# Deep and own blocks of a sparse graph attention in turns, and several steps of its schedule queued elsewhere

## The chip, the cores and the metric

The kernel runs on one core of a Trainium2 chip. That core has five engines: TensorE (PE, with its weight loads shown apart as PEld), VectorE (DVE), ScalarE (ACT), GpSimd (POOL) and SyncE (SP, which here issues transfers only). The metric is the time of one execution on the device in microseconds (us), as the median of several runs.

## The reference

It is one layer of multi-head attention over a fixed graph, with a residual and a layer norm: 16 batches of 1024 nodes with 512 features, 8 heads of 64, everything in float32. The adjacency `adj` (1024 x 1024, zeros and ones) is the same for all batches and sparse, and its rows have very different lengths.

```python
q = (x @ Wq + bq).reshape(b, n, H, HD)
k = (x @ Wk + bk).reshape(b, n, H, HD)
v = (x @ Wv + bv).reshape(b, n, H, HD)
scores = jnp.einsum('bqhd,bkhd->bhqk', q, k) / jnp.sqrt(jnp.float32(HD))
scores = scores + (1.0 - adj)[None, None, :, :] * -1000000000.0
attn = jax.nn.softmax(scores, axis=-1)
out = jnp.einsum('bhqk,bkhd->bqhd', attn, v).reshape(b, n, d)
x = _layernorm(x + out @ Wo + bo, axis=-1)
```

A row without any neighbour gets the average of all v. The random graph is an input, so the kernel finds its neighbours on the chip.

## The kernel before

**Tiles and blocks.** The 1024 nodes are ranked by their number of neighbours and cut into 8 tiles of 128. Instead of a dense product of scores, the kernel walks over neighbours: a *block* is 128 pairs of a query and a key. For a block, POOL gathers the keys' rows of k and v (1024 numbers each, tile `kvg`) from memory, DVE multiplies q with k (`products`, L1251) and adds up each head (`scores`, L1255), ACT takes the exponentials (`exponentials`, L1266), and v is multiplied with them (`weigh`): by ACT in eight small instructions, one for each head (L1276), or by DVE in one (L1280). `by_act` says which.

There are two kinds. In an *own* block every partition holds one of its own queries (the i-th neighbour of each), so that DVE simply adds it to the tile's sum (`add_own`, L1292); the first one of a tile starts the sum. `OWN = (2, 1, 2, 3, 4, 5, 5, 7)` gives their number by tile. What longer rows have beyond that is packed into *deep* blocks, `BLOCKS = (0, 0, 0, 0, 0, 0, 1, 5)`. A deep block's partitions belong to arbitrary queries, so it needs a second gather (`qg`, L1184), and PE adds it up with a matrix of zeros and ones (`add_up`, L1301 and L1302, into a PSUM tile with one buffer). A batch has 32 or 34 blocks, all batches together 530. Tile 1 has one key and no blocks. From batch 2 on, batches go in pairs: the odd one ("merged") also does the tile 0 of both.

**The written-out schedule.** The order of the instructions on every engine comes from one loop over steps `n` (L1470 on), some 39 steps ahead of block 0 up to 12 after the last. Each engine then runs its own instructions in that order and waits for the others by semaphores. In step n the loop queues the exponentials of block n+3, the products of n+4, gathers up to block n+8 (`AHEAD`; 11 ahead once the fronts are done), DVE's weighing of n+1, ACT's of n+2, and the sum of n. `later(k, fn)` puts a piece of work k steps ahead. The gathers of a batch may only be queued once `set_up` has the batch.

**PE's units.** PE's products are cut into units, with a credit for each step (`share`, paced by `load_of`). `fronts` are the projections of coming batches: `pair(b, j)` does q, k and v for two tiles of x. The k and v products follow a scheme with seven half products for eight, in units of four PE records: x, p6, x again, p7, z, p4, z again. Banks x and z have one buffer, and the second use waits for ACT's copy `e` (L960) or DVE's `out_v1` (L975). Between them stand the query products `q0` and `q1` (`pq`, L790) and the transposes `xt` of coming x tiles (`pxT`, L748). `finish` is the output product of a tile (`po`, also L790), and `complete` its residual and layer norm: spread (ACT), variance (DVE), power (POOL, L1113), shift (DVE), norm_out (ACT), store (POOL, L1125). `urgent` holds single PE pieces that go ahead of units: transposes of finished tiles and `mean_pe` (`pm`, L858), the average of v. Its row is copied by ACT (L862) and stored by SP (L864), and that is what sets `set_up`.

**What the change also touches.** `load_x` gathers a tile of x (L1001; three buffers) on POOL. `bias_setup` and `edges` are generators that run one piece at each step, in the lead-in: they fold bv into the output's bias (`pb`, L419) and make the lists of the deep blocks (`poff`, L675). The y tiles of `complete` have six buffers. While fronts last, kvg has eight.

Of the kernel before, what the change touches and what calls it, by code (L numbers as in the profile page):

```python
# [177 lines left out]
def kernel(  # L178
# [37 lines left out]
    B, N, D = x.shape  # L216
# [37 lines left out]
    with ExitStack() as main:  # L254
# [139 lines left out]
        def bias_setup():  # L394
            bk_bc = work.tile([P, D], F32, tag="y", name="bk_bc", bufs=Y_BUFS)
            broadcast(bk_bc, bk)
            yield
            n4 = small.tile([P, NPAIR], F32, name="bk_norms", bufs=1)
            nc.vector.tensor_tensor(bk_bc, bk_bc, bk_bc, op=OP.mult)
            nc.vector.tensor_reduce(n4, bk_bc.rearrange("p (h d) -> p h d", d=P), axis=AX.X, op=OP.add)  # L400
            nc.vector.tensor_reduce(bk_norm, n4, axis=AX.X, op=OP.max)
            n8 = small.tile([P, HEADS], F32, name="bq_norms", bufs=1)
            nc.vector.tensor_tensor(bk_bc, bq_bc, bq_bc, op=OP.mult)
            nc.vector.tensor_reduce(n8, bk_bc.rearrange("p (h d) -> p h d", d=HD), axis=AX.X, op=OP.add)
            nc.vector.tensor_reduce(bq_norm, n8, axis=AX.X, op=OP.max)
            yield
            pb = fill_psum("pb")
            nc.tensor.transpose(pb[:, 0:2 * NPAIR], bias_rows, ident[:2 * NPAIR, :2 * NPAIR])
            nc.tensor.transpose(pb[:, 2 * NPAIR:3 * NPAIR], bv_rows, ident[:NPAIR, :NPAIR])
            yield  # L410
            nc.vector.tensor_copy(bias_qk, pb[:, 0:2 * NPAIR])
            bv_col = one.tile([P, NPAIR], F32, name="bv_col")
            nc.vector.tensor_copy(bv_col, pb[:, 2 * NPAIR:3 * NPAIR])
            bvb = work.tile([P, NPAIR, P], F32, tag="y", name="bvb", bufs=Y_BUFS)
            nc.vector.tensor_copy(bvb, bv_col[:, :, None].to_broadcast([P, NPAIR, P]))
            yield
            pb = fill_psum("pb3")
            for c in range(NPAIR):
                nc.tensor.matmul(pb, bvb[:, c, :], W["o"][:, c, :], start=(c == 0), stop=(c == NPAIR - 1))  # L419
            yield  # L420
            nc.vector.tensor_tensor(bo_bc, pb, bo_bc, op=OP.add)
# [20 lines left out]
        def later(k, fn):  # L442
            plan.setdefault(now[0] + k, []).append(fn)
# [187 lines left out]
        def edges(t):  # L631
# [38 lines left out]
                nc.vector.tensor_tensor(check[:, 2 * NT + 1:2 * NT + 2], ranked[:, t, 1:2], st[:, 0:1], op=OP.subtract)  # L670

            nc.vector.tensor_scalar(deg, ranked[:, t, 1:2], -float(K), 0.0, op0=OP.add, op1=OP.max)
            yield
            po = fill_psum(f"poff_{t}")
            nc.tensor.matmul(po[:, 0:1], before, deg, start=True, stop=True)  # L675
            yield
# [66 lines left out]
        def transpose_x(b, t):  # L743
            def pe():
                xs = X.pop((b, t))
                p = fill_psum(f"pxT_{b}_{t}")
                for c in range(NPAIR):
                    nc.tensor.transpose(p[:, ts(c, P)], xs[:, ts(c, P)], ident)  # L748

                def out():  # L750
                    XT[b, t] = work.tile([P, D], F32, tag="xT", name=f"xT_{b}_{t}", bufs=4)
                    nc.scalar.copy(XT[b, t], p)
                    n = b * NT + t + 3
                    if t == 0 and b >= PAIRED_FROM:
                        if not merged(b):
                            BOTH[b // 2] = work.tile([P, 2, NPAIR, P], F32, tag="place", name=f"both_{b}", bufs=1)
                        nc.scalar.copy(
                            BOTH[b // 2].rearrange("p w c (h n) -> p h c w n", h=2)[:, b % 2],
                            p.rearrange("p (c w n) -> p c w n", c=NPAIR, w=2),
                        )  # L760
                        sq = work.tile([P, D], F32, tag="ysq", name=f"sq_x_{b}", bufs=1)
                        nc.scalar.activation(sq[0:LONE, :], xs[0:LONE, :], AF.Square, accum_out=x_norm[0:LONE, b:b + 1])
                    if b * NT + t in STORED:
                        nc.sync.dma_start(residual[b * NT + t], xs)
                        later(2, lambda: load_x(n // NT, n % NT))
                    else:
                        load_x(n // NT, n % NT)
                    if t % 2 and (b, t) != (0, 1):
                        later(1, combine)

                def combine():
                    s = [work.tile([P, HD2], F32, tag=f"s{i}", name=f"s{i}_{b}_{t}", bufs=1 + i // 4) for i in (1, 2, 3, 4)]
                    x0, x1 = XT[b, t - 1], XT[b, t]
                    nc.vector.tensor_tensor(s[0], x1[:, 0:HD2], x1[:, HD2:D], op=OP.add)
                    nc.vector.tensor_tensor(s[2], x0[:, 0:HD2], x1[:, 0:HD2], op=OP.subtract)
                    nc.vector.tensor_tensor(s[1], s[0], x0[:, 0:HD2], op=OP.subtract)
                    nc.vector.tensor_tensor(s[3], x0[:, HD2:D], s[1], op=OP.subtract)
                    SX[b, t // 2] = s

                later(1, out)  # L780

            return [(TRANSPOSE, pe, lambda: (b, t) in X)]
# [24 lines left out]
        def pair(b, j):  # L807
# [25 lines left out]
            def send(i):  # L833
# [8 lines left out]
                if R["sent"] == 2:  # L842
                    later(1, add_v)
                    if j == NT // 2 - 1:
                        later(2, lambda: urgent.append(mean_pe))

            def add_v():
                kv = [KV.pop((b, t))[:, D:] for t in tt]
# [133 lines left out]
            def s(i):  # L982
                return lambda: SX[b, j][i - 1]

            units = []
            units += unit("x", lambda: a(0, 0), B11, True, out_e, None)
            units += unit("p6", s(2), T2, True, out_w, None)
            units += q0
            units += unit("x", lambda: a(0, 1), B21, False, lambda: out_k(0, R["x"]), "e")
            units += unit("p7", s(3), T3, True, out_g, None)  # L990
# [94 lines left out]
        def complete(b, t, p, plain):  # L1085
# [46 lines left out]
            if single:  # L1132
                late = 1 if fronts else 0
                later(2 + late, variance)
                later(3 + late, power)
                later(4 + 2 * late, shift)
                later_last(5 + 2 * late, norm_out)
            elif second:
                later(3, variance)
                mate_shift, mate_norm_out = half.pop()[1]  # L1140
# [29 lines left out]


        KG, QG, PV, PSUM, QT, RDEN, V1 = {}, {}, {}, {}, {}, {}, {}
        blocks = [(b, t, i) for b in range(B) for t in tiles_of(b) if t != ONE_KEY for i in range(OWN[t] + BLOCKS[t])]
        start = [min(n for n, block in enumerate(blocks) if block[0] == b) for b in range(B)] + [len(blocks)]

        def load_more():
# [90 lines left out]

        def by_act(n):
            b, t, i = blocks[n]
            return 0 < i < OWN[t] or n < total - NBT and (n % 2 == 0 or n < NBT // 2)  # L1270

        def weigh(n):
            v, pv = KG.pop(n), PV[n]
# [174 lines left out]
        with tc.manual_schedule():  # L1448
# [21 lines left out]
            while n < total or plan or rest or urgent or done or finishing or spilled or lone_tiles or not guarded:  # L1470
# [50 lines left out]
                    reload(*spilled.pop(0), reloads)  # L1521
                    reloads, last_reload = reloads + 1, n
                first_unit = True
                while credit > 0 or urgent:
                    if urgent and not (first_unit and fronts):
                        urgent.pop(0)()
                        continue
                    if (
# [2 lines left out]
                    ):  # L1531
                        finishing = finish(*done.pop(0))
                        last_finish = n
                    units = finishing or fronts
                    if not units:
                        if urgent:
                            urgent.pop(0)()
# [52 lines left out]
```

## Time and profile before

| | us |
|---|---|
| median of 3 runs | 1903.44 (1902.83 to 1912.35) |
| the profiled execution | 1892.33 |
| its span, first to last instruction | 1890.4 |
| mean granted TensorE clock | 0.989 |
| PE / DVE / ACT / POOL busy | 1815.1 / 1700.6 / 1531.7 / 1267.4 |

The profile is of one execution. Busy time is the union of an engine's instructions; idle time in front of an instruction is put down to whatever released it last. In a row of the waits, the first number is the total in us, then follow how often, and the longest. The row of a group ends with its busy time, the mean ns of one instruction, and the idle time before them. All rows of PE count two records for one float32 matrix product.

### The profile page before, as it was taken

Reading aid. Unit: us, or ns where it says so; the run is one execution under the profiler, and the core shown is the slowest. Engines: PE = TensorE matmul, PEld = TensorE weight load, DVE = VectorE, ACT = ScalarE, POOL = GpSimd, SP = SyncE. Lnnn points to the kernel's source line nnn. Section 1 sums busy time; section 2 is a strip of 40 time slices with the busy share of each in tenths; the row PEclk is TensorE's granted clock in tenths of the full one; section 3 lists DMA queues with packets and bytes.
Section 4 is the critical chain, followed back from the end, with each engine's and each line's share of the span. In section 5 each row is a group of like instructions: output and inputs, shape, how many; then the busy total and the mean of one; then the engine's idle time right before and its main releaser. Section 6 shows DMA issues by size and latency. Waiting matters only on the chain. (4 is left out here: it accounts for less than half of the span.)

```text
span 1890.4 us, 25101 instructions
## 1 busy us (share of the span) xinstructions
PE 1815.1 (96%) x5149; PEld 878.2 (46%) x5149; DVE 1700.6 (90%) x3484; ACT 1531.7 (81%) x6016; POOL 1267.4 (67%) x1189
## 2 busy tenths in 40 slices
PE   7989999999999999999999999999999999999995
PEld 3434444444545454444445444444445444444442
DVE  6888889999999999899899989899999999997874
ACT  3627869979888988979798978989898989886794
POOL 1367766777677676757677676767666777656774
PEclk9989999999999999999999999999999999999997
DMA  7357787988889898888889898999889899989993
GB/s 280 114 168 226 233 307 227 315 295 294 308 287 316 305 328 283 305 288 307 312 292 335 271 334 274 314 304 310 301 307 326 293 356 310 314 277 340 334 319 117
DMA packets 188149, 544.63 MB, mean 288 GB/s; under 512 B 32602, under 2 KB 32622, under 8 KB 187986
## 3 DMA queue, kind: packets, MB, share of 16 engines
q0 software_dynamic: 116400, 382.82, 60.6%
q1 hardware_dynamic: 68510, 154.30, 21.8%
q10 hardware_dynamic: 3076, 5.82, 0.9%
q14 instruction: 120, 0.98, 0.2%
q8 instruction: 43, 0.70, 0.1%
HBM read 419.52 MB, written 144.34 MB: 298 GB/s over the span
## 5 line engine op out<-in xcount | busy, mean ns | idle before, releaser
L1276 ACT ACTIVATE pv<-kvg,pv 128x64 f32<-128x64 f32 x3432 | 864.6, 340 | 0.0
L1230 POOL DMA_INDIRECT kvg<-kv_pair,place_row x462 | 526.7, 1140 | 258.0 <-ACT pv L1276 73.3
L790 PE MATMUL po<-wo,oT 128*128 128x512 f32 x816 | 380.1, 596 | 1.0 <-ACT oT L1340 0.9
L790 PE MATMUL pq<-wq,xT 128*128 128x512 f32 x792 | 368.9, 597 | 0.4 <-DVE g L966 0.4
L1255 DVE TENSOR_REDUCE s<-qk 128x8 f32<-128x512 f32 x530 | 360.2, 680 | 7.5
L1251 DVE TENSOR_TENSOR qk<-qt,kvg 128x512 f32<-128x512 f32 x434 | 296.4, 683 | 22.2 <-DMA kvg<-kv_pair,place_row 22.1
L947 PE MATMUL pp<-t,s 128*128 128x512 f32 x504 | 237.4, 593 | 2.7 <-ACT sq_k L800 1.7
L947 PE MATMUL x<-b,xT 128*128 128x512 f32 x504 | 237.8, 594 | 0.8 <-ACT e L960 0.8
L790 PEld LDWEIGHTS po<-wo,oT 128*128 128x128 f32 x816 | 152.6, 191 | 166.8 <-issue 153.9
L1292 DVE TENSOR_TENSOR pv<-pv,pv 128x520 f32<-128x520 f32 x329 | 228.0, 693 | 0.7 <-ACT pv L1276 0.6
L790 PEld LDWEIGHTS pq<-wq,xT 128*128 128x128 f32 x792 | 149.2, 192 | 166.4 <-issue 155.0
L1266 ACT ACTIVATE pv<-s,absent 128x8 f32<-128x8 f32 x434 | 126.3, 293 | 79.8 <-DVE s L1255 76.2
L1001 POOL DMA_INDIRECT x<-in_x_dram,asked_row x120 | 130.2, 1085 | 88.3 <-PE pxT L748 40.5
L1125 POOL DMA_INDIRECT out_dram<-y,asked_row x129 | 144.8, 1122 | 35.7 <-issue 19.8
L800 ACT ACTIVATE sq_k<-kv 128x128 bf16<-128x128 f32 x512 | 150.9, 301 | 6.0 <-DVE kv L970 6.0
L947 PEld LDWEIGHTS pp<-t,s 128*128 128x128 f32 x504 | 94.2, 190 | 114.1 <-issue 101.4
L947 PEld LDWEIGHTS x<-b,xT 128*128 128x128 f32 x504 | 94.3, 191 | 111.5 <-issue 106.5
L1184 POOL DMA_INDIRECT qg<-q_rows,query_row x96 | 106.9, 1114 | 36.5 <-issue 24.7
L947 PE MATMUL z<-b,s 128*128 128x512 f32 x252 | 119.1, 595 | 6.5 <-DVE kv L975 6.5
L1029 POOL DMA_INDIRECT y<-in_x_dram,asked_row x93 | 104.5, 1124 | 27.5 <-issue 25.8
L947 PE MATMUL z<-t,s 128*128 128x512 f32 x252 | 120.0, 599 | 0.0
L947 PE MATMUL pp<-t,xT 128*128 128x512 f32 x252 | 118.4, 592 | 0.0
(276 smaller groups left out, 2766.7 us busy)
## 6 DMA issues: line engine op xcount, KB each, us to landing
kv_pair<-kv SPq DMA_DIRECT2D x98, 512.0 KB
q_rows<-q SPq DMA_DIRECT2D x106, 256.0 KB
qt<-q_rows SPq DMA_DIRECT2D x98, 256.0 KB
residual<-x SPq DMA_DIRECT2D x36, 256.0 KB
y<-residual SPq DMA_DIRECT2D x36, 256.0 KB
kv_rows<-kv SPq DMA_DIRECT2D x15, 512.0 KB
kvg<-kv_pair,place_row POOLq DMA_INDIRECT x462, 6.5
kv_pair<-kv SPq DMA_DIRECT2D x28, 256.0 KB
```

The source lines that it names most:

```text
L790: nc.tensor.matmul(p, lhs(c), w[:, c, :], start=(c == 0), stop=(c == NPAIR - 1))
L800: nc.scalar.activation(sq, s[:, ts(h, P)], AF.Square, scale=scale, accum_out=sums[:, h:h + 1])
L947: nc.tensor.matmul(R[bank], l[:, ts(c, P)], right[:, c, :], start=(first and c == 0), stop=(c == 1), skip_group_check=True,)
L1001: nc.gpsimd.indirect_dma_start(out=y, out_offset=None, in_=x_rows, in_offset=bass.IndirectOffsetOnAxis(ap=asked_row[:, t:t + 1], axis=0), ...
L1125: nc.gpsimd.indirect_dma_start(out=out_rows[b, t], out_offset=bass.IndirectOffsetOnAxis(ap=rows, axis=0), in_=y, in_offset=None, element_o ...
L1184: nc.gpsimd.indirect_dma_start(out=q, out_offset=None, in_=q_rows[b % ROWS], in_offset=bass.IndirectOffsetOnAxis(ap=rows, axis=0))
L1230: nc.gpsimd.indirect_dma_start(out=KG[n], out_offset=None, in_=rows, in_offset=bass.IndirectOffsetOnAxis(ap=(place_row if b else key_row)[ ...
L1251: nc.vector.tensor_tensor(QK[n], q, KG[n][:, 0:D], op=OP.mult)
L1255: nc.vector.tensor_reduce(S[n], QK.pop(n).rearrange("p (h d) -> p h d", d=HD), axis=AX.X, op=OP.add)
L1266: nc.scalar.activation(PV[n][:, D:], S.pop(n), AF.Exp, bias=bias)
L1276: nc.scalar.activation(pv[:, ts(h, HD)], v[:, ds(D + h * HD, HD)], AF.Copy, scale=pv[:, D + h:D + h + 1])
L1292: nc.vector.tensor_tensor(PV[b, t], PV[b, t], pv, op=OP.add)
```

## The change

Eight edits:

- `blocks_of`: in batches 1 to 15 the deep blocks of a tile are put between its own blocks, tile 7 as 0 1 D 2 D 3 D 4 D 5 D 6, tile 6 as 0 1 2 D 3 4. The first block of a tile stays first.
- `by_act`: a deep block's engine now goes by the parity of batch and number (`b + i`) instead of the parity of its place in the whole order.
- the product of the average of v is queued four steps after the second v tile instead of two;
- `bias_setup` and `edges` wait two steps more ahead of their products;
- a gather of x is queued one step later;
- in `complete`, while fronts last, power, shift and norm_out are queued one step later;
- in each batch's first pair, one x transpose takes the place of the first query product, and the query products and the other transpose stand between z's two uses;
- in the last three steps that have blocks, no units are queued, only urgent pieces.

```diff
--- before.py
+++ after.py
@@ -413,7 +413,8 @@
             nc.vector.tensor_copy(bv_col, pb[:, 2 * NPAIR:3 * NPAIR])
             bvb = work.tile([P, NPAIR, P], F32, tag="y", name="bvb", bufs=Y_BUFS)
             nc.vector.tensor_copy(bvb, bv_col[:, :, None].to_broadcast([P, NPAIR, P]))
-            yield
+            for _ in range(3):
+                yield
             pb = fill_psum("pb3")
             for c in range(NPAIR):
                 nc.tensor.matmul(pb, bvb[:, c, :], W["o"][:, c, :], start=(c == 0), stop=(c == NPAIR - 1))
@@ -670,7 +671,8 @@
                 nc.vector.tensor_tensor(check[:, 2 * NT + 1:2 * NT + 2], ranked[:, t, 1:2], st[:, 0:1], op=OP.subtract)
 
             nc.vector.tensor_scalar(deg, ranked[:, t, 1:2], -float(K), 0.0, op0=OP.add, op1=OP.max)
-            yield
+            for _ in range(3):
+                yield
             po = fill_psum(f"poff_{t}")
             nc.tensor.matmul(po[:, 0:1], before, deg, start=True, stop=True)
             yield
@@ -764,7 +766,7 @@
                         nc.sync.dma_start(residual[b * NT + t], xs)
                         later(2, lambda: load_x(n // NT, n % NT))
                     else:
-                        load_x(n // NT, n % NT)
+                        later(1, lambda: load_x(n // NT, n % NT))
                     if t % 2 and (b, t) != (0, 1):
                         later(1, combine)
 
@@ -842,7 +844,7 @@
                 if R["sent"] == 2:
                     later(1, add_v)
                     if j == NT // 2 - 1:
-                        later(2, lambda: urgent.append(mean_pe))
+                        later(4, lambda: urgent.append(mean_pe))
 
             def add_v():
                 kv = [KV.pop((b, t))[:, D:] for t in tt]
@@ -985,6 +987,8 @@
             units = []
             units += unit("x", lambda: a(0, 0), B11, True, out_e, None)
             units += unit("p6", s(2), T2, True, out_w, None)
+            if j == 0:
+                q0, q1, xt = xt[:1], q0 + xt[1:], []
             units += q0
             units += unit("x", lambda: a(0, 1), B21, False, lambda: out_k(0, R["x"]), "e")
             units += unit("p7", s(3), T3, True, out_g, None)
@@ -1132,9 +1136,9 @@
             if single:
                 late = 1 if fronts else 0
                 later(2 + late, variance)
-                later(3 + late, power)
-                later(4 + 2 * late, shift)
-                later_last(5 + 2 * late, norm_out)
+                later(3 + 2 * late, power)
+                later(4 + 3 * late, shift)
+                later_last(5 + 3 * late, norm_out)
             elif second:
                 later(3, variance)
                 mate_shift, mate_norm_out = half.pop()[1]
@@ -1170,7 +1174,19 @@
 
 
         KG, QG, PV, PSUM, QT, RDEN, V1 = {}, {}, {}, {}, {}, {}, {}
-        blocks = [(b, t, i) for b in range(B) for t in tiles_of(b) if t != ONE_KEY for i in range(OWN[t] + BLOCKS[t])]
+
+        def blocks_of(b, t):
+
+            own, deep = list(range(OWN[t])), list(range(OWN[t], OWN[t] + BLOCKS[t]))
+            if b == 0 or not deep:
+                return own + deep
+            spread = max(1, len(own) // (len(deep) + 1))
+            left = len(own) - spread * len(deep)
+            for j, i in enumerate(deep):
+                own.insert(left + j * (spread + 1), i)
+            return own
+
+        blocks = [(b, t, i) for b in range(B) for t in tiles_of(b) if t != ONE_KEY for i in blocks_of(b, t)]
         start = [min(n for n, block in enumerate(blocks) if block[0] == b) for b in range(B)] + [len(blocks)]
 
         def load_more():
@@ -1267,7 +1283,10 @@
 
         def by_act(n):
             b, t, i = blocks[n]
-            return 0 < i < OWN[t] or n < total - NBT and (n % 2 == 0 or n < NBT // 2)
+            if 0 < i < OWN[t]:
+                return True
+            turn_of = b + i if b and i else n
+            return n < total - NBT and (turn_of % 2 == 0 or n < NBT // 2)
 
         def weigh(n):
             v, pv = KG.pop(n), PV[n]
@@ -1521,7 +1540,8 @@
                     reload(*spilled.pop(0), reloads)
                     reloads, last_reload = reloads + 1, n
                 first_unit = True
-                while credit > 0 or urgent:
+                last_sums = total - 3 <= n < total
+                while credit > 0 and not last_sums or urgent:
                     if urgent and not (first_unit and fronts):
                         urgent.pop(0)()
                         continue
@@ -1531,7 +1551,7 @@
                     ):
                         finishing = finish(*done.pop(0))
                         last_finish = n
-                    units = finishing or fronts
+                    units = [] if last_sums else finishing or fronts
                     if not units:
                         if urgent:
                             urgent.pop(0)()
```

## The prediction before the run

> **What bounds the kernel now.** I read the page's busy table first, then busy time by stage, then the waits of TensorE (PE), and last who holds up the engines that PE waits for.
>
> ```profile
> PE 1815.1 (96%) x5149; PEld 878.2 (46%) x5149; DVE 1700.6 (90%) x3484; ACT 1531.7 (81%) x6016; POOL 1267.4 (67%) x1189
> ...
> L1276 ACT ACTIVATE pv<-kvg,pv 128x64 f32<-128x64 f32 x3432 | 864.6, 340 | 0.0
> ...
> kvg<-kv_pair,place_row POOLq DMA_INDIRECT x462, 6.5
> ```
>
> PE is the bound, with VectorE (DVE) close behind. The stages (PE, PEld, DVE, ACT, POOL busy; then clock, DMA share, GB/s):
>
> ```profile
> 0.00:136.00 136.00, 116.16 (x316) 54.05 (x317) 105.06 (x255) 60.17 (x168) 48.44 (x67) 0.98 0.53 187
> 136.00:275.00 139.00, 138.66 (x384) 66.01 (x383) 116.15 (x236) 104.02 (x435) 105.11 (x98) 0.98 0.76 246
> 275.00:1741.00 1466.00, 1433.48 (x4107) 698.09 (x4106) 1377.21 (x2704) 1266.77 (x5105) 1012.84 (x929) 1.00 0.88 304
> 1741.00:1891.00 150.00, 126.79 (x346) 60.04 (x344) 102.14 (x291) 100.78 (x311) 101.04 (x97) 0.93 0.73 263
> ```
>
> PE idles 19.8 us before the first block, 0.3 in batch 0, 32.5 in batches 1 to 14 (462 blocks, 3.17 us each) and 23.2 in the last batch and the end: 75 us. No edit takes a product away from PE, so those 75 us are the ceiling. What ends PE's waits, and DVE's and POOL's:
>
> ```profile
> PE sum L1301 <- DVE pv L1280: 13.8, 6, 3.7
> PE z L947 <- DVE kv L975: 6.5, 6, 2.4
> PE pm L858 <- DVE vsum L854: 5.6, 4, 1.9
> PE pb L419 <- DVE bvb L415: 5.6, 1, 5.6
> PE poff L675 <- DVE est L672: 2.1, 1, 2.1
> ...
> DVE qk L1251 <- DMA kvg<-kv_pair,place_row: 25.6, 13, 4.9
> ...
> POOL kvg L1230 <- ACT pv L1276: 88.0, 72, 6.2
> POOL x L1001 <- PE pxT L748: 40.5, 19, 13.6
> POOL stats L1113 <- DVE stats L1110: 29.6, 19, 4.3
> POOL qg L1184 <- DVE qk L1251: 9.4, 6, 4.3
> ```
>
> PE's five rows are 33.6 us, and each belongs to an edit. The sum waits stand at the seams of batches: at 806 us DVE had waited 4.3 us for the next batch's gathered rows, and PE then 3.75 us for DVE. Those gathers are late because eight of them are in flight in eight buffers: block n+8's gather waits until block n is weighed, and in tiles 6 and 7 ScalarE (ACT) weighs 12 of 13 blocks in a row, after which five deep blocks each want a second gather (qg).
>
> **What the Trainium skill says.** "Perfetto Trace Analysis", Identifying the Most-Contended Engine, warns that matmul busy time doesn't tell how near the roofline is. Here the chain of waits has eight records of pq in 3.43 us, 0.429 each; the some 3,620 records of 512 columns make 1,553 us at that pace, transposes, sums and the rest some 230, so PE is at its pace and the trace agrees with its busy row. The same page, Optimization Strategy, advises interleaving regimes whose most-contended engine differs: the alternation does this. "PSUM — Partial Sum Buffer", Engine vs sequencer instructions: ACT, DVE and GpSimd queues are strict FIFO. The trace agrees: one x gather held POOL 13.6 us. "DMA: Bandwidth & Descriptors", Anatomy of one DMA — SWDGE (gpsimd) path, prices a gather at 2.0 us and bytes over 436 GB/s, 3.2 us for 512 KB (an estimate); the page above has 6.5 us to landing under this load, and I use that.
>
> **The change part by part** (against the profiled execution, span 1890.4 us, 1892.33 with what lies around it).
>
> *List and bias products later.* Two steps more ahead of poff and pb; PE runs its products meanwhile. PE is without idle in batch 0, so what is saved ahead of it stays saved. Removed 5.6 + 2.1 = 7.7 us; the waits are shorter than the two steps, but DVE is still late with neighbours: I take **-6** (0 to -7.7).
>
> *Pair's last products apart.* In each batch's first pair only the fourth matrix product (1.72 us) stood between the two uses of bank z, while DVE reads z out (0.69 us and its queue). Now one x transpose (0.44 us) or, in merged batches, the query products (3.44 us and 0.9) stand there too. In exchange the query products leave the place between p6 and the second use of bank x, where PE waits for ACT's copy e. Unmerged batches already have nothing there, and the whole kernel's wait of that kind is 0.8 us. Removed 6.5, given back up to 1.5: **-5** (-6.5 to +2).
>
> *Average of v later.* The product pm moves two steps (6.3 us) behind the additions, longer than its longest wait: **-5.5** (-7 to 0, with 1.3 us that the group's idle adds). The cost: the row of averages gates the next batch's gathers. Around batch 15 (ACT copy, SP's store, POOL's first gather, its product on DVE):
>
> ```profile
> 1727.63 0.56 ACT L862 COPY mean<-pm 1x512 f32<-1x512 f32 x1
> ...
> 1728.21 0.24 SPq L864 DMA_DIRECT2D kv_pair<-mean  x1
> ...
> 1731.80 1.04 POOL L1230 DMA_INDIRECT kvg<-kv_pair,place_row  x1 [0.30 <-issue]
> ...
> 1738.68 0.69 DVE L1251 TENSOR_TENSOR qk<-qt,kvg 128x512 f32<-128x512 f32 x1
> ```
>
> Working the scheduler's loop through for both files gives the step at which a batch is released: 420, 456, 488 for batches 13, 14, 15, now 423, 458, 490. Their first blocks are 430, 464, 496, so the first gather, otherwise 8 steps ahead, is now 6, 5, 5. The product is queued 4 steps ahead of its block; 2, 1, 1 steps (6.3, 3.2, 3.2 us) are left for 6.5 us of landing. In earlier batches the release is still early enough. Batch 14's first product waited 2.9 us before; 15's had 1.2 us to spare. I expect DVE to stall some 1, 6 and 4 us, net of the 2.9 +8 on DVE; behind its product queue the weighing, PE's sums and the pair's additions. At the seams of the trace about 0.7 of such a stall reaches PE, in batch 15 little, since po products of stored tiles lie ready: **+4** (0 to +10).
>
> *Deep and own blocks alternate.* The five deep blocks of tile 7 lie between own blocks, tile 6's after its third. So qg gathers come every second block, and the blocks that ACT weighs no longer stand in one run. Of the sum waits, 11 us are ahead of the end, 4.7 of them after even batches, whose count on ACT stays (2 of 6 deep). But for odd batches 1 to 13 the parity rule puts 4 of 6 on ACT. One costs 8 x 0.252 us (864.6 / 3432) = 2.0 us of ACT against 0.68 on DVE: +28 us of ACT and -9.6 of DVE in all. Where this lands, the last 18 blocks of odd batches 3 to 13 (columns as above):
>
> ```profile
> sum 326.10, PE 311.99 PEld 150.12 DVE 297.66 ACT 300.06 POOL 239.57; mean PE 52.00 PEld 25.02 DVE 49.61 ACT 50.01 POOL 39.93
> ```
>
> ACT there goes from 50.0 of 54.4 us to 54.0 of 54.4. It can carry some 4 us of lateness into the next batch, where it has room, but kvg buffers come free later by as much. Gain **-6** from the sum waits (-11 to 0), loss **+5** (0 to +28).
>
> *x gathers and powers later.* 120 gathers go one step later on POOL, past gathers of kvg and lookups; the eight direct loads keep their order on SP. Powers (while fronts last) go one step, shift and normalisation with them, so y buffers are held a step longer; of six, the gate admits five. POOL loses up to 40.5 + 29.6 us of waiting, but it is at 67% and isn't the bound: counted in the kvg term, else **0** (-4 to +3). A tile of x is wanted some 12 steps later, which covers the step.
>
> *Last sums.* In the last three steps no product stands ahead of the sums. Before, eight products of two tiles did, at 1860 to 1865.8 us, and PE idled 5.5 us among the last waits. Afterwards three tiles (10.3 us) are left for PE behind the sums, two of them beside the normalising of the last tile: **-3** (-5 to +4).
>
> Sum: -6 -5 -5.5 +4 -6 +5 -3 = **-16.5**. About a fifth of the waits removed will appear again at the next thing that is late, as DVE and ACT are over 90% busy in these stretches: **-13**, a span of 1877. The three runs' median, 1903.44, lies 11 us above the profiled execution; in the same ratio (0.993), **1890**.
>
> **The rivals.** *A slower kernel: ACT becomes the bound of tiles 6 and 7 in odd batches.* The stretch has 54.4 us; it decides from the point where ACT's own needs, 54.0 us, and the waits it can't avoid (4.3 us idle now, for PE's bank x and transposes) no longer fit, and the next batch can't take up the rest because kvg gathers wait for ACT (88 us already). If each of seven pays its 4 us, the +5 above is +28 and the sum +10; with the late release at its worst, +16: 1913 to 1920. For it: the POOL row above. Against it: DVE waits only 0.6 us for ACT's weighing in the whole trace.
>
> *No change: waits trade places.* Only the lead-in and the tail pay (-9), the seams lose as much as pm and z win, +6: about -3, 1900. For it: DVE at 94% in the even stretches. *All targeted waits go and nothing is paid:* 7.7 + 6.5 + 7 + 11 + 3, less the fifth, -28: 1875.
>
> **How the numbers follow.** A measurement tells about 0.5%, 9.5 us, from no change. The forecast and the good rival, below 1894: 0.56. Waits that trade places, or gains that just cancel ACT's cost, 1894 to 1913: 0.25. ACT as a bound, or late gathers worse than thought: 0.19. The range 1870 to 1918 leaves out some 2 in 10; the likeliest case alone has 1880 to 1898.
>
> **What would show it.** Right: PE's rows pb, poff, pm <- vsum and z <- kv under 1 us each; sum <- pv at most 5; DVE's waits for kvg at 1520 to 1740 us longer than before, but shorter elsewhere; ACT 1560 busy, DVE 1691. Wrong: ACT's stretches of odd batches at 99% and longer than 55 us, new rows of DVE or PE waiting for ACT's pv, or a lead-in as long as before.

## The result and the profile after

| | us | ratio to the kernel before |
|---|---|---|
| before, measured beside it, 22 runs | 1910.16 (1900.32 to 1923.28) | |
| after, 22 runs | 1915.63 (1904.32 to 1926.93) | 1.0024 [1.0007, 1.0041] |
| profiled execution of after / its span | 1916.64 / 1914.9 | |

The changed kernel is slower by 0.24%, where I forecast 0.7% faster (1890, against 1903.44). From one group of runs to another the kernel before itself took 1890.6 to 1925.3 us, so times are compared as ratios within a group, and the shown profile of before (1892.33) belongs to the low end of that while the one of after (1916.64) belongs to the middle.

The page of after, its busy row and the row of ACT's weighing:

```profile
PE 1825.8 (95%) x5147; PEld 881.0 (46%) x5147; DVE 1698.7 (89%) x3472; ACT 1558.2 (81%) x6128; POOL 1266.3 (66%) x1189
...
L1295 ACT ACTIVATE pv<-kvg,pv 128x64 f32<-128x64 f32 x3544 | 893.3, 339 | 1.2 <-issue 1.0
```

ACT got the 112 instructions (14 blocks) and the 28 us that were forecast, and is still at 81%. PE is 10.7 us busier with the same products. Busy time by stage (lead-in, batch 0, batches 1 to 14, last batch and end; PE, PEld, DVE, ACT, POOL, then clock, DMA share, GB/s):

```profile
0.00:134.20 134.20, 119.10 (x322) 55.99 (x323) 105.53 (x256) 60.08 (x169) 48.80 (x67) 0.97 0.54 190
134.20:286.50 152.30, 139.48 (x377) 65.14 (x376) 116.36 (x235) 104.39 (x434) 103.09 (x98) 0.96 0.71 230
286.50:1767.40 1480.90, 1445.33 (x4121) 702.74 (x4119) 1370.78 (x2683) 1288.79 (x5206) 1008.00 (x927) 0.99 0.87 300
1767.40:1915.00 147.60, 121.89 (x330) 57.09 (x329) 106.05 (x300) 104.91 (x323) 106.44 (x99) 0.93 0.75 267
```

The lead-in is 2 us shorter than before and the last stage 2 us. Batch 0, in which PE had no idle time, is 13.3 us longer: PE idles 12.8 us there and its clock is 0.96. Batches 1 to 14 are 14.9 us longer, with 35.6 us of PE idle time (32.5 before) and a clock of 0.99 instead of 1.00. Not all of this is the change's doing, as the two profiles come from different groups; the section after this one separates the two. The waits of PE, and the ones of DVE and POOL that answer to those of before:

```profile
PE sum L1320 <- DVE pv L1299: 10.2, 7, 4.6
PE pp L949 <- DVE s L777: 8.7, 3, 5.0
PE pxT L750 <- DMA x<-in_x_dram: 6.6, 2, 3.7
PE x L949 <- ACT e L962: 5.7, 4, 3.9
PE pp L949 <- DVE s L778: 5.0, 1, 5.0
PE z L949 <- issue: 4.7, 3, 2.5
PE pp L949 <- ACT oT L1359: 4.6, 1, 4.6
PE pp L949 <- DVE kl L680: 4.4, 1, 4.4
PE z L949 <- DVE kv L977: 3.8, 3, 1.4
...
DVE qk L1267 <- DMA kvg<-kv_pair,place_row: 18.4, 9, 6.0
DVE est L679 <- remote: 6.5, 1, 6.5
...
POOL kvg L1246 <- ACT pv L1295: 104.5, 68, 6.2
```

The rows pb and pm are gone from PE, and 0.8 us is left of poff. z waits 3.8 us for kv instead of 6.5, but another 4.7 us with no recorded releaser (issue). In their place stand rows that before did not have at that size: pp waiting 13.7 us for DVE's combinations `s` of x, x for ACT's copy e, pp behind the list work (kl).

### The profile page after: what moved, and what is told of

Read it like the earlier page. It is cut to its first block, busy times and chain, and to the rows that moved or that the text cites. A ratio compares the mean times of both kernels' runs of the same rounds, so it can differ in the third digit from the quotient of the medians.

```text
span 1914.9 us, 25163 instructions
## 1 busy us (share of the span) xinstructions
PE 1825.8 (95%) x5147; PEld 881.0 (46%) x5147; DVE 1698.7 (89%) x3472; ACT 1558.2 (81%) x6128; POOL 1266.3 (66%) x1189
## 5 line engine op out<-in xcount | busy, mean ns | idle before, releaser
L1295 ACT ACTIVATE pv<-kvg,pv 128x64 f32<-128x64 f32 x3544 | 893.3, 339 | 1.2 <-issue 1.0
L792 PE MATMUL po<-wo,oT 128*128 128x512 f32 x816 | 373.7, 593 | 1.8 <-ACT oT L1359 1.4
L949 PE MATMUL pp<-t,s 128*128 128x512 f32 x504 | 243.5, 606 | 18.6 <-DVE s L777 8.7
L949 PE MATMUL z<-b,s 128*128 128x512 f32 x252 | 123.2, 612 | 9.2 <-issue 4.7
L1200 POOL DMA_INDIRECT qg<-q_rows,query_row x96 | 102.8, 1071 | 32.8 <-issue 25.8
```

Source lines behind the costliest of these rows:

```text
L792: nc.tensor.matmul(p, lhs(c), w[:, c, :], start=(c == 0), stop=(c == NPAIR - 1))
L949: nc.tensor.matmul(R[bank], l[:, ts(c, P)], right[:, c, :], start=(first and c == 0), stop=(c == 1), skip_group_check=True,)
L1295: nc.scalar.activation(pv[:, ts(h, HD)], v[:, ds(D + h * HD, HD)], AF.Copy, scale=pv[:, D + h:D + h + 1])
```

## Where the time lies: waits of PE, and what the clock adds

One sum holds for every profile of this study. Take from the span PE's idle time up to its last product, the stretch after that product, and half of the time that PE was busy at the half clock. What is left is PE's work at full clock:

| profile | span | PE idle | after its last product | half-clock loss | left |
|---|---|---|---|---|---|
| before | 1890.4 | 61.6 | 13.7 | 13.9 | 1801.2 |
| after | 1914.9 | 73.7 | 15.4 | 24.3 | 1801.5 |
| after again, group 3 (e9) | 1902.3 | 67.1 | 15.4 | 18.6 | 1801.2 |
| after again, group 4 (e13) | 1876.4 | 51.0 | 15.4 | 12.9 | 1797.2 |
| alternation alone (e5) | 1878.9 | 56.2 | 13.7 | 9.4 | 1799.6 |

Over all 20 profiles the last column lies between 1797 and 1805. So after's 24.5 us above before are 12.1 us of PE waits, 1.7 us at the end, and **10.4 us of clock that the waits brought with them**. No term of the prediction had a clock.

But much of this belongs to the group and not to the change. e11 and e12 are the kernel before with one edit each that leaves its time as it is, and were timed where before took 1908.79 us: they have 68.3 and 75.7 us of PE idle time and 12.4 and 12.1 us of half-clock loss, and their batch 0 takes 145.1 and 147.4 us. What the change adds is seen within a group. Every timed run has its mean granted clock on record. One minus the clock, times the span, is the time lost to it (means over all runs, in us; standard errors of 0.4 to 1.1):

| group | kernel | runs | span | lost to the clock | rest |
|---|---|---|---|---|---|
| 3 | before | 71 | 1907.3 | 23.4 | 1883.9 |
| 3 | e9, the whole change | 22 | 1911.2 | 28.8 | 1882.3 |
| 3 | e10, four of its edits undone | 18 | 1893.1 | 19.0 | 1874.1 |
| 4 | before | 29 | 1888.4 | 20.6 | 1867.8 |
| 4 | e13, the whole change | 7 | 1876.6 | 19.0 | 1857.6 |

In group 3 the change leaves the rest as it was, within the error, and adds **5.4 us of half clock**; without four of its edits both fall. In group 4 it takes 10.2 us off the rest and 1.6 off the clock.

Here is what a wait costs behind itself in one place, PE around a wait of 4.64 us in batch 8 (start, duration, engine, line, operation):

```profile
1107.16 3.75 PE L949 MATMUL pp<-t,s 128*128 128x512 f32 x4 [4.64 <-ACT oT L1359]
...
1115.61 1.88 PE L949 MATMUL x<-b,xT 128*128 128x512 f32 x4
```

```profile
1107.16:1110.71 3.55, 3.55 (x5) 1.49 (x6) 2.80 (x5) 3.43 (x12) 2.94 (x3) 0.50 0.98 336
1115.61:1117.33 1.72, 1.72 (x5) 0.76 (x4) 1.72 (x4) 0.00 (x0) 1.41 (x2) 1.00 0.95 364
```

Four records right after the wait take 3.75 us at a clock of 0.50; the same four take 1.88 at 1.00 a few microseconds later. The wait cost 4.64 us, and the clock behind it another 1.9 in this unit alone.

## The experiments

Eighteen runs in five groups. Each was timed beside the kernel before in the same group; those times were 1907.88 (group 1), 1890.86 (2), 1908.79 (3), 1890.57 (4) and 1925.33 us (5). The theory at the start: the alternation gains, and single edits give it back by waits of their own. The rivals: the late release of batches 13 to 15, or ACT's larger share in odd batches, ate the gain.

### Group 1: one edit of the changed kernel undone

e1, the pair's last products where they were:

```diff
-            if j == 0:
-                q0, q1, xt = xt[:1], q0 + xt[1:], []
```

> The changed kernel with one edit undone: in a batch's first pair the transposes and query products stand where they stood before (both x transposes ahead of z, query products between p6 and the second use of x). Theory A (the second x transpose now comes too late for the next pair's combination s1 to s4, and the query products no longer cover ACT's copy e): PE's waits of pp for DVE's s (13.7 us in the changed kernel's profile) and of x for e (5.7) fall under 3 together, z for kv returns to some 6, TensorE's half-clock time falls by 20 us; faster than the changed kernel by 8 to 15 us, ratio to the kernel before 0.994 to 0.998. Theory B (late release of batches 13 to 15 is what ate the gain): pp's waits go, but the time stays within 3 us of the changed kernel, ratio about 1.001. Theory C (ACT's larger share in odd batches): as B.

Measured: 1.0018 [0.9999, 1.0036]. PE's waits:

```profile
PE z L949 <- DVE kv L977: 13.9, 6, 4.9
PE sum L1318 <- DVE pv L1297: 11.0, 7, 4.5
PE pq L792 <- DVE bo_bc L422: 8.2, 1, 8.2
```

The rows pp<-s are gone and z<-kv is back, at 13.9 for 13.7: idle in all 73.8 us against 73.7. The edit trades one wait for another of the same size.

e2, the average of v two steps after the additions again:

```diff
-                        later(4, lambda: urgent.append(mean_pe))
+                        later(2, lambda: urgent.append(mean_pe))
```

> The changed kernel with the product of the average of v queued two steps after the second v tile, as before. Theory A: DVE's stalls at the first products of batches 13 to 15 (4.1, 4.5 and 6.0 us) go down to 3 at one of them, but the pp waits stay; ratio 1.000 to 1.002. Theory B: with those stalls PE's waits at 1556, 1656 and 1772 us (3.2, 1.9 and 4.6) and their half-clock stretches go; pm waits for vsum return with some 6 us; ratio 0.995 to 0.998. Theory C: no change, 1.002.

Measured: 1.0016 [0.9992, 1.004]. Not to be told from the whole change, though in its profile DVE's stalls at the first products of batches 14 and 15 fall to 2.0 and 1.2 us, and none of over 0.9 us is left at batch 13.

e3, the old order of blocks and the old split, all other edits kept:

```diff
-            if b == 0 or not deep:
+            if True:
...
-            turn_of = b + i if b and i else n
+            turn_of = n
```

> The changed kernel with own blocks first and deep blocks last in every tile, and the old rule for the engine that weighs (2 of 6 deep blocks on ACT); the rest stays. Theory A: the sum waits at the seams of even batches return (+5 us), ACT loses 28 us of work which was not on the path; slower than the changed kernel by 2 to 6 us, ratio 1.004 to 1.006. Theory C (the alternation with ACT's larger share in odd batches costs more than it gives): faster than the changed kernel, ratio 0.995 to 1.000, odd batches shorter by 2 us each.

Measured: 1.0064 [1.0041, 1.0086]. The only one of the four that moves: without the alternation the rest of the change costs 0.64%.

e4, list and bias products after one step again, at both places:

```diff
-            for _ in range(3):
-                yield
+            yield
```

> The changed kernel with the products pb and poff one step after their inputs, as before. If the two steps more are what lengthened the lead-in and batch 0 (134 and 152 us against 136 and 139 in the profile before, where DVE waits 6.5 us for poff and PE 4.4 us for what follows it), batch 0 comes down to about 142 us and the ratio to 0.997 to 0.999. If batch 0 is longer because of the transposes in the first pair (theory A), it stays at 148 to 152 us, the waits pb and poff return (7 us), and the ratio is 1.002 to 1.005.

Measured: 1.0021 [1.0004, 1.0038]. The lead-in is 3.3 us longer than in after (137.5 against 134.2) and batch 0 7.2 us shorter (145.1 against 152.3), and the time shows no gain from the edit. That it is lost in batch 0 holds for these two profiles alone: e13 below has the edit and a batch 0 of 135.6 us.

### Group 2: the alternation alone, its split, x gathers, powers

e5, the kernel before with `blocks_of` and the new `by_act`, and nothing else:

```diff
-        blocks = [(b, t, i) for b in range(B) for t in tiles_of(b) if t != ONE_KEY for i in range(OWN[t] + BLOCKS[t])]
+        blocks = [(b, t, i) for b in range(B) for t in tiles_of(b) if t != ONE_KEY for i in blocks_of(b, t)]
...
+            turn_of = b + i if b and i else n
```

> The kernel before with only the alternation of deep and own blocks and the new rule for the weighing engine. If the other six edits together are what costs (the run with the order put back had a ratio of 1.0064, and they are all that it has), this is faster than the kernel before: ratio 0.994 to 0.998, batch 0 at 139 us as before. If the alternation and the other edits only work together, ratio 1.000 or more. Odd batches 1 to 13 sum to some 760 us (746 before) if ACT's larger share in them costs, even ones to 714.

Measured: 0.9921 [0.9903, 0.9939], 1877.38 us. PE's row of sums is down from 13.8 us to

```profile
PE sum L1316 <- DVE pv L1295: 6.4, 4, 2.6
```

e6, the changed kernel with two of six deep blocks on ACT in every batch (four of six in odd ones is what the change has):

```diff
-            turn_of = b + i if b and i else n
+            turn_of = i if b and i else n
```

> The changed kernel with deep blocks weighed on ACT by the parity of their number alone: 2 of 6 in every batch, so the old count in odd batches too. Theory C (ACT's larger share holds the odd batches up): odd batches 1 to 13 fall from 761 us to about 748, ACT's busy time by 28 us; ratio 0.996 to 0.999. If the odd batches are longer because of the new order itself or of late gathers: they stay at 757 or more, ratio 1.002 to 1.004.

Measured: 0.9987 [0.9978, 0.9996], 1889.33 us. That lies in theory C's range, but the range was reckoned from the 1.0024 of the result. Beside e13 in group 4 (0.9933, at the same time of before) the kernel with the old count on ACT is the slower one.

e7, x gathers not later; e8, powers not later:

```diff
-                        later(1, lambda: load_x(n // NT, n % NT))
+                        load_x(n // NT, n % NT)
```

```diff
-                later(3 + 2 * late, power)
-                later(4 + 3 * late, shift)
-                later_last(5 + 3 * late, norm_out)
+                later(3 + late, power)
+                later(4 + 2 * late, shift)
+                later_last(5 + 2 * late, norm_out)
```

> The changed kernel with the gathers of x in the step of the transposes, as before. If the later gathers of x are what makes tiles of x and so PE's combined operands late (pp waits for DVE's s in batch 0 and in the middle), those waits fall under 5 us, batch 0 comes to 145 us or less, ratio 0.998 to 1.000. If the step was covered, as the prediction has it: ratio 1.002 to 1.004, POOL's waits for pxT back at 40 us.

> The changed kernel with power, shift and norm_out in the steps of before. If the longer chain of the layer norm holds y buffers and so the output products back, PE's po units come earlier and the ratio is 0.998 to 1.001. If it is neutral: 1.002 to 1.004, with POOL's wait for the variance (stats) back at some 30 us.

Measured: 0.9963 [0.9941, 0.9984] and 0.9933 [0.9913, 0.9954]. Against the 1.0024 of the result both looked like cures. They were not: the whole change was not in this group, and the next groups show what it does there.

### Group 3: the whole change again, four edits undone, two edits alone

e9 is the changed kernel as it is. e10 undoes pair, average, x gathers and powers, by the diffs of e1, e2, e7 and e8 together, and so keeps alternation, lists and last sums. e11 is the kernel before with

```diff
-                later(3 + late, power)
-                later(4 + 2 * late, shift)
-                later_last(5 + 2 * late, norm_out)
+                later(3 + 2 * late, power)
+                later(4 + 3 * late, shift)
+                later_last(5 + 3 * late, norm_out)
```

and e12 the kernel before with

```diff
-                        load_x(n // NT, n % NT)
+                        later(1, lambda: load_x(n // NT, n % NT))
```

> The changed kernel, unaltered, as a control beside the next three runs; across calls the time of the kernel before itself moved by 1%, so that the earlier ratios need one. Theory A (the alternation gains some 0.8%, the other edits give it back, whatever the day): ratio 1.001 to 1.004, some 0.9 to 1.1% above the alternation alone. Theory B (the loss belongs to the condition of the first call, in which batch 0 takes 145 to 153 us): ratio 0.992 to 0.996 where batch 0 takes 135 to 139 us, so that single edits cost next to nothing.

> The changed kernel with four edits undone: the pair's last products, the average of v, the x gathers and the powers are where they were. Left are the alternation with its split, the list and bias products two steps later and the last sums. Theory A: the gain of the alternation (0.8%) and some 6 us of PE's waits in the lead-in: ratio 0.988 to 0.992, no PE row pb or poff, none pp<-s over 3 us. Theory B (the edits left here cost what they save, since what is saved ahead of batch 0 is lost in it): the ratio of the alternation alone or worse, 0.992 to 0.996.

> The kernel before with the powers, shift and normalisation of a finished tile one step later each, and nothing else. Theory A (the later powers hold y buffers and the normalising behind the next tile, and so cost by themselves): ratio 1.003 to 1.006. Rival (they cost only beside the pair's edit, by the order of POOL's queue): ratio 0.999 to 1.001, no PE row pp<-s over 2 us.

> The kernel before with the x gathers one step later on POOL's queue, and nothing else. Theory A (a later gather makes a later combination and so a later first half of a pair, with PE waiting for DVE's s): ratio 1.001 to 1.004, PE's row pp<-s over 5 us. Rival (a tile of x is wanted so much later that the step is covered): ratio 0.999 to 1.001, POOL's wait x<-pxT (40.5 us in the kernel before) below 20, nothing new on PE.

Measured: e9 1.0025 [1.0005, 1.0045]; e10 0.9929 [0.991, 0.9947]; e11 0.9988 [0.9972, 1.0004]; e12 1.0011 [0.9993, 1.0028]. So in this group the four edits together cost 1.0%, and neither powers nor x gathers cost that alone. e10 is faster than both kernels, by 0.7% and 1.0%. It was expected to have no row pb, as it keeps the later list and bias products, and it has one:

```profile
PE pb L420 <- DVE bvb L415: 6.5, 1, 6.5
```

So two steps more don't remove that wait by themselves.

### Group 4: the whole change again, and pairs of edits undone

e13 is the changed kernel as it is, e14 repeats e8, e15 undoes x gathers and powers (diffs of e7 and e8), e16 x gathers and the pair's edit (e7 and e1).

> The changed kernel again, unaltered, as the control of this call. Theory A (four edits cost 1% together, in every condition): 1.001 to 1.004. Rival (the loss shows only where the kernel before takes 1908 us): 1.002 to 1.004 if before takes 1908 us here, 0.994 to 0.998 if it takes 1891 us.

> The changed kernel with the powers, shift and normalisation at their old steps. Theory P (the later powers, behind the later x gathers on POOL and with a y buffer held longer, carry the loss): 0.6 to 0.9% under the control. Rival X (x gathers with the pair's edit carry it): 0 to 0.3% under the control.

> The changed kernel with x gathers and powers both at their old steps; what stays is alternation, pair, average, lists, last sums. Theory P: no better than powers undone alone, 0.6 to 0.9% under the control. Theory PX (the two meet on POOL's queue, each costs a half): 0.9 to 1.1% under the control, near 0.993. Rival X: about 0.3 to 0.5%.

> The changed kernel with x gathers and the pair's last products as before. Rival X (a later gather and a later second transpose add up to a later combination, and the fronts are not ready): 0.8 to 1.1% under the control, PE's row pp<-s gone. Theory P: 0 to 0.4% under the control, since the powers are still late.

Measured: e13 **0.9933** [0.991, 0.9957], 1878.3 us; e14 0.9933 [0.9907, 0.996]; e15 0.9936 [0.9912, 0.9959]; e16 0.9972 [0.996, 0.9983]. The rival of e13 holds: where before takes 1891 us, the changed kernel is 0.7% faster, and the later powers, alone or with the later x gathers, are worth nothing in it. e16 met neither theory: with x gathers and the pair's edit undone the kernel is 6.7 us *slower* than e13 (1884.98 against 1878.3, intervals just apart), so these two together gain here. (e7, x gathers undone alone, took 1884.01 in group 2, so that which of the two earns it is not separated.) PE's waits in e13:

```profile
PE sum L1320 <- DVE pv L1299: 9.7, 6, 4.5
PE pp L949 <- DVE s L778: 9.4, 5, 5.0
...
PE z L949 <- DVE kv L977: 3.2, 2, 2.6
```

Batches 0 to 14 of the same kernel in e13:

```profile
133.90:269.50 135.60, 134.98 (x381) 64.49 (x380) 115.75 (x235) 103.92 (x434) 103.13 (x98) 1.00 0.79 259
269.50:1729.70 1460.20, 1434.74 (x4112) 700.39 (x4119) 1370.33 (x2683) 1286.16 (x5206) 1003.63 (x928) 1.00 0.88 305
```

Beside the profile of after: 16.7 and 20.7 us shorter, with 0.6 instead of 12.8 us of PE idle time in batch 0. The row of z with its second product, in e16 and in e13:

```profile
L949 PE MATMUL z<-b,s 128*128 128x512 f32 x252 | 122.8, 610 | 10.2 <-DVE kv L977 10.0
L949 PE MATMUL z<-b,s 128*128 128x512 f32 x252 | 119.2, 595 | 3.2 <-DVE kv L977 3.2
```

### Group 5: the four edits split two and two

e17 is e15 again; e18 is the changed kernel with the pair's edit and the average undone (diffs of e1 and e2).

> The changed kernel with x gathers and powers at their old steps (alternation, pair, average, lists and last sums stay). If before takes 1908 us: theory P (work that was put later on POOL's queue has no slack left when transfers are late) 0.993 to 0.996; rival M (the pair's edit and the average, which bring PE and DVE to wait for each other, carry the loss) 1.000 to 1.003. If before takes 1891 us: 0.992 to 0.995, as in the run before.

> The changed kernel with the pair's last products and the average of v as before (alternation, x gathers, powers, lists and last sums stay). If before takes 1908 us: theory P 1.000 to 1.003, rival M 0.993 to 0.996. If before takes 1891 us: 0.992 to 0.997, no PE row pp<-s over 3 us, rows pm and z<-kv back.

Measured: before took 1925.33 us, more than in any other group; e17 0.9942 [0.9923, 0.9961], e18 0.9953 [0.993, 0.9975]. Both halves alone give most of e10's gain. Either it takes all four edits to lose it, or this group differs from group 3; the whole change was not in it, so this stays open.

e15 and e17 are one kernel at 1874.8 and 1918.2 us of span: 29.7 us more PE idle time and 10.8 us more half-clock loss. One place in e17 where engines stop, around 217 us:

```profile
213.42 0.31 ACT L802 ACTIVATE sq_k<-kv 128x128 bf16<-128x128 f32 x1 [0.34 <-issue]
...
214.13 0.20 ACT L802 ACTIVATION_READ_ACCUMULATOR sq_k<-kv 128x1 f32 x1 [0.40 <-issue]
...
217.72 0.31 ACT L802 ACTIVATE sq_k<-kv 128x128 bf16<-128x128 f32 x1 [2.66 <-remote]
217.72 0.69 DVE L1103 TENSOR_TENSOR y<-po,y 128x512 f32<-128x512 f32 x1 [9.91 <-remote]
217.97 1.00 POOL L1246 DMA_INDIRECT kvg<-kv_rows,key_row  x1 [0.30 <-remote]
```

ACT stops 2.66 us in the middle of a series on one tile that it had begun, and DVE 9.91 us, although PE's last product for it ended at 210.2; both go on in the same hundredth of a microsecond. The trace has ACT's instruction waiting only for a counter that ACT itself raises, and the last of its instructions that raises it had ended at 215.06. In e15 the same ACT series runs without a gap, and DVE's instruction follows its product after a wait of 2.23. The row `DVE est L679 <- remote` of after (6.49 us at 151.15; 5.03 at 151.35 in e9) is such a place too, in batch 0, and PE's wait of 4.4 us for kl follows it; in e13 this instruction waits for nothing. The profile names no releaser for these stops ("remote", "issue"). Waits put down to "remote" stand in every profile of the groups in which before took 1907 us or more, and in none of groups 2 and 4 or of before. But in those groups it also records over a third fewer semaphore events (some 15,600 landings in e9, 25,300 in e13), so that part of these rows may be releasers that went unrecorded. What stops the engines, and how much of the time it takes, is not settled by these runs.

## Why the prediction was wrong

Measured against the profile of before, which belongs with groups 2 and 4:

| step | forecast, us | shown by | measured |
|---|---|---|---|
| lists and bias later | -6 | rows pb, poff; e4; e10 | rows gone in e13 (-7.7); e4 sees no gain in the time; e10 has the edit and 6.5 of pb |
| pair's last products | -5 | e13's rows; e1; e16 | z<-kv -3.3, pp<-s +9.4 beside before; e1: waits of 13.9 for 13.7, same time; with x gathers -6.7 (e16 against e13) |
| average later | -5.5 | row pm | gone (-5.6) |
| late release of batches 13 to 15 | +4 | PE idle beside DVE's stalls | 9.7 in after, 2.5 in before: +7.2 |
| alternation, sums | -6 | e5's row | -7.4 |
| alternation, ACT's larger share | +5 | e6 against e13 | -11 |
| x gathers, powers | 0 | e11, e12; e14, e15 beside e13 | 0 (e7 and e16 leave up to -6 for x gathers open) |
| last sums | -3 | e3, e5 | none seen |
| clock after waits | not priced | clocks of all runs | +5.4 in group 3, -1.6 in group 4 |

**The transfer of the total failed.** Where before is as fast as in its profile, the total is met: in group 4 the change gives 1878.3 against 1890.57, -12.3 us, and the forecast was -13. The step that failed is the last one of the sum: "The three runs' median, 1903.44, lies 11 us above the profiled execution; in the same ratio (0.993), 1890". Those 11 us are no common factor. The profiled 1892.33 lay outside the range of the three runs, 1902.83 to 1912.35, so the waits and the slack were read from an execution unlike the ones that the forecast was for. Where before takes 1908.79 us, the same change has a ratio of 1.0025 (e9), and without four of its edits 0.9929 (e10). All four put work later, and slack was counted on to cover it. That stops like the one of e17 use up this slack is my reading and is not shown. Nor is it shown how each of the four takes part, as no single one of them costs 1% (e1, e2, e11, e12).

**That the total fits in group 4 is luck.** The alternation with its split alone gives 13.5 us at such a time of before (e5, 1877.38 against 1890.86), and the sum had -1 for it (-6 and +5). The other six edits had -15.5, and together give about nothing: 0.9933 with them (e13), 0.9921 without (e5). The waits show it too. Of the 33.6 us in PE's five rows e13 has 12.9 left, so 20.7 went; but PE's idle time fell only from 61.6 to 51.0. About half came back at other waits, where I had taken a fifth.

**Pair.** The prediction never asked who was waiting for the transposes that were moved. DVE's combinations `s` for the next unit need both. With the second transpose behind z, `s` comes late; e1, with the transposes back, has no such row. The first case costs 5.03 us at 125.9 us of after, 4.96 at 125.6 of e13, still in the lead-in; there DVE had been busy with the bias norms and started `s` at 124.4. That is a part of why the lead-in gained 2 us and not 6: e13's takes 133.9 us, e16's, with the transposes back, 132.4. Beside before, e13's two rows say +6.1, past my range of -6.5 to +2. But before is the wrong kernel to set them beside, as the alternation alone lengthens the wait of z to 8.5 us (e5). In the changed kernel the edit trades waits without effect on the time in e1 (the rival "waits trade places"), and in e16 undoing it, with the x gathers, costs 6.7 us.

**Late release.** The mechanism held and its size was too small. Batch 15's average, SP's store, POOL's first gather and DVE's product in after:

```profile
1755.56 0.56 ACT L864 COPY mean<-pm 1x512 f32<-1x512 f32 x1
1756.14 0.24 SPq L866 DMA_DIRECT2D kv_pair<-mean  x1
...
1759.82 1.02 POOL L1246 DMA_INDIRECT kvg<-kv_pair,place_row  x1 [0.31 <-issue]
...
1765.93 0.69 DVE L1267 TENSOR_TENSOR qk<-qt,kvg 128x512 f32<-128x512 f32 x1 [5.98 <-DMA kvg<-kv_pair,place_row]
...
1772.17 1.22 PE L1320 MATMUL sum<-pv,sums 128*128 128x256 f32 x2 [4.59 <-DVE pv L1299]
```

I had 1, 6 and 4 us of DVE stalls for batches 13, 14 and 15; they were 4.08, 4.46 and 5.98. PE paid 3.24, 1.90 and 4.59 us at those seams, 9.7 in all, where before had paid 2.51 at batch 14's, so some 7 more; the argument that stored tiles keep PE going in batch 15 was wrong. The 5.5 us won at pm are lost here, which fits e2, whose time is that of the whole change.

**Alternation.** The sum waits went as forecast. ACT's share had the wrong sign. e6 has the whole change but for that share, and takes 1889.33 where e13 takes 1878.3, in two groups whose times of before differ by 0.3 us. By the means over all runs 6.2 us of it are in the rest and 4.0 in the clock. A likely reason is that PE waits for DVE more than for ACT (in e13 9.7 us for pv and 9.4 for s, against 4.6, 1.9 and 1.0 in ACT's rows), so that taking work off DVE pays; no run shows this by itself. The last 18 blocks of odd batches 3 to 13 in after:

```profile
sum 336.20, PE 319.05 PEld 155.10 DVE 296.28 ACT 309.24 POOL 239.31; mean PE 53.17 PEld 25.85 DVE 49.38 ACT 51.54 POOL 39.88
```

ACT is busy 51.5 of 56.0 us there, not 54.0 of 54.4. The stretch became longer, which looked like a sign of the rival "ACT becomes the bound"; but at 92% it is not ACT that fills it, and e13 has 54.45 us for it with 51.2 of ACT. e6, with less on ACT, has 53.4 us there: the larger share lengthens these stretches by 1 us each, and the gain lies elsewhere. That rival is out, though the time it gave, 1913 to 1920, is the one that was measured.

**What I got right:** x gathers and powers cost nothing by themselves (1.0011 and 0.9988); the rows pb, pm, poff go in e13; ACT at 1558 for 1560 forecast. The last sums show no gain: e5 doesn't have them, and its last stage takes 145.1 us; e3 has them without the alternation, and 152.7. In e13, with both, it is 146.8 against 150 in before, so the forecast -3 came with the alternation.

## What to carry to other kernels

Where PE is the bound, price a wait of more than 2 us with what it costs behind itself, and write the sum as work plus waits plus clock: that shows at once whether an edit removed a wait or moved it. Before a step is put later, list who needs its result, and test the slack against a run that is a per cent slower than the profile, since a gain that rests on slack of a few microseconds may not be there on another run. See that the profile from which a forecast is made is of an execution like those that it is for. And repeat the kernel itself in each group of experiments: without e9 and e13, e7 and e8 would have been read as cures.

## What the runs showed of the hardware

The granted clock of TensorE is halved around waits much shorter than I had thought to matter, and in whole steps: up to PE's last product 95 stretches of half clock took 3.41 us, 47 took 6.83, 4 took 10.24 and one 17.07. In the 20 profiles, from the first record of the clock on (11 to 14 us), of PE's waits of 3.5 us and more, 60 of 60 had half-clock time within 4 us after them; of those of 2 to 3.5 us, 68 of 118 (37 of 66 up to 2.5); of 1.6 to 2 us, 21 of 86; of 0.3 to 1.6 us, 22 of 444. The Trainium skill, "TensorE: Matmul & The Clock Gate", section "Why this matters for your kernels", advises no PE-idle gaps over some 3 us; its section "What's actually happening" gives a free-running window of 3413 ns. The lengths agree with that window. The threshold is lower here: waits of 2 to 3.5 us were followed by half clock more often than not, and where PE is busy all through it, it costs 1.7 us (half of 3.41) or more each time, about half of such a wait or more.
